# A fill of an unused tile after every gather on GpSimd, in a recommender kernel

## The chip, the cores and the metric

The kernel runs on one core of a Trainium2 chip. The metric is the device time of one execution in microseconds (us). The kernel before takes 5192.12 us, the median of three runs (5191.66 to 5192.24).

## The reference

The reference is a wide-and-deep recommender for a batch of 16384 examples. Each example looks up 32 rows of 300 floats in a table of 50000 words and takes their mean; it looks up 20 rows in each of three smaller tables (means) and one row in each of four small ones. The 748 features go through three dense layers, and a sum of scalar weights is added ahead of the sigmoid.

```python
tok = word_emb[token_idx].mean(axis=1)            # 32 rows of 300 floats
e1 = emb_mh1[mh1_idx].mean(axis=1)                # 20 rows of 64, also e2 and e3
o1 = emb_oh1[oh1_idx]                             # one row of 64, also o2, o3 and o4
emb = jnp.concatenate([tok, e1, e2, e3, o1, o2, o3, o4], axis=1)
wide = (wide_mh1[mh1_idx].sum(axis=(1, 2)) + ... + wide_oh4[oh4_idx][:, 0])[:, None]
h = jax.nn.relu(emb @ W1 + b1)                    # 748 -> 1024
h = jax.nn.relu(h @ W2 + b2)                      # 1024 -> 512
h = jax.nn.relu(h @ W3 + b3)                      # 512 -> 256
return jax.nn.sigmoid(h @ Wd + bd + wide)         # 256 -> 1
```

## The kernel before

The batch is cut into 128 tiles of 128 examples. Two streams of work run beside each other for each tile.

The token rows come from HBM. GpSimd issues one indirect DMA for each of the 32 token positions of a tile: 128 rows of 1200 bytes, one for each partition, 4096 gathers in all. Two gathers share one row buffer, and there are eight row buffers. VectorE adds the two halves of a buffer to a running sum in PSUM, three groups after the gathers of that buffer were issued.

```python
TOK_GROUP = 2
TOK_LAG = 3
TOK_BUFS = 8
...
tokp = ctx.enter_context(tc.tile_pool(name="tok", bufs=TOK_BUFS))
...
def add_up(t, q, rows):
    a, b = rows[:, 0:TOK_D], rows[:, TOK_D : 2 * TOK_D]
    if q == 0:
        nc.vector.tensor_add(tok_sum, a, b)
    else:
        nc.vector.tensor_add(tok_sum, tok_sum, a)                  # L216
        to = tok_sum
        if q == n_groups - 1:
            to = sums_of[t] = gp.tile([P, TOK_D], F32, name="g_tok")
        nc.vector.tensor_add(to, tok_sum, b)                       # L220

def tokens():
    under_way = []
    for n in range(n_all):
        if n < n_all - TOK_LAG:
            t, q = divmod(n, n_groups)
            it = token_indices[t // NSUB][:, t % NSUB, :].bitcast(U32)
            rows = tokp.tile([P, TOK_GROUP * TOK_D], F32, name="tok_rows")
            for r in range(TOK_GROUP):
                j = q * TOK_GROUP + r
                nc.gpsimd.indirect_dma_start(                      # L232
                    out=rows[:, r * TOK_D : (r + 1) * TOK_D],
                    out_offset=None,
                    in_=word,
                    in_offset=bass.IndirectOffsetOnAxis(ap=it[:, j : j + 1], axis=0),
                )
            under_way.append((t, q, rows))
        if n >= TOK_LAG:
            add_up(*under_way.pop(0))
        yield 1
```

The small tables are kept on chip. VectorE builds one-hot rows (L299), TensorE turns them into counts in PSUM tile `pc` (L317), ACT copies the counts to SBUF as fp8 (L324), and TensorE multiplies the counts with the tables into PSUM tile `pg` (L342). Every tile's features are then transposed by TensorE, tile by tile (`pt`), and the dense layers run on blocks of 256 examples (`ph`, L419, and the last layer `po`, L444).

The order of all this is written by hand: a loop over 11 steps per tile, and 16 steps more at the end, sends out a share of each stream in every step. The token groups are spread evenly over these steps, so that the groups of a tile drift against the tile's other work.

```python
n_steps = tiles * STEPS + WAKE
...
for step in range(n_steps):
    ...
    toks.to(n_all * (step + 1) / n_steps)
    for k in set(sums_of) - known:
        waiting.append((step + 2, Block.add_tokens, k, sums_of.pop(k)))
    ...
    if layers:
        layers.to(mlp_work * layers.size * (step + 1 - begin) / left + ahead)
```

Apart from four one-column constants, the identity for transposes and one row of numbers, GpSimd does nothing but these gathers.

Of the kernel before, what the change touches and what calls it, by code (L numbers as in the profile page):

```python
# [8 lines left out]
F32 = mybir.dt.float32  # L9
# [8 lines left out]
P = 128  # L18
# [4 lines left out]
TOK_GROUP = 2  # L23
TOK_LAG = 3
TOK_BUFS = 8
WAKE = 16
BLOCK = 512
LAYER_TILES = 2
# [20 lines left out]
def kernel(  # L49
# [21 lines left out]
    nc = tc.nc  # L71
# [11 lines left out]

    tokp = ctx.enter_context(tc.tile_pool(name="tok", bufs=TOK_BUFS))
    const = ctx.enter_context(tc.tile_pool(name="const", bufs=1))
# [108 lines left out]
    def load_weights():  # L194
# [7 lines left out]
        for sb, dram in ((wd_sb, wd), (b1_sb, b1), (b2_sb, b2), (b3_sb, b3), (bd_sb, bd)):  # L202
            nc.sync.dma_start(out=sb, in_=dram)

    n_groups = N_TOK // TOK_GROUP
    n_all = B // P * n_groups + TOK_LAG
    sums_of = {}
# [2 lines left out]
# [11 lines that stand above are left out]

    def tokens():

        under_way = []
        for n in range(n_all):
            if n < n_all - TOK_LAG:
# [8 lines that stand above are left out]
                        in_=word,  # L235
                        in_offset=bass.IndirectOffsetOnAxis(ap=it[:, j : j + 1], axis=0),
                    )
                under_way.append((t, q, rows))
            if n >= TOK_LAG:
                add_up(*under_way.pop(0))  # L240
            yield 1
# [255 lines left out]
    tiles = B // P  # L497
    n_steps = tiles * STEPS + WAKE
    mlp_work = NK * M1 + M1 * M2 + M2 * M3 + M3
# [19 lines left out]
    ctx.enter_context(tc.manual_schedule())  # L519
    ix = load_indices(0)  # L520
    toks = Paced(tokens())
    tables_on_chip = convert_tables()
    next(tables_on_chip)
# [96 lines left out]
```

## Time and profile before

| what | value |
|---|---|
| timed runs | 5192.12 us (median of 3) |
| the profiled execution | 7640.41 us, of which the span shown is 7638.6 us |
| mean granted TensorE clock in the profile | 0.875 |
| gathers | 4096, 629.41 MB in 196608 packets |
| share of 16 DMA engines that the gathers' packets took | 30.4% |

The profiled execution is much longer than the timed ones. So the durations of single instructions and the distances between them can be read from the profile, while shares of its span hold for that span alone. In the groups of the profile, each line gives the source line, the engine and the operation, what is written and read, the count, and then the busy time in us, the mean of one in ns, and the idle time of the engine just before, with what ended most of it. PE is TensorE's matmuls, PEld its weight loads, DVE is VectorE, ACT ScalarE and POOL GpSimd. In a timeline each line begins with the start and the duration in us.

### The profile page before, as it was taken

The numbers are of one execution on the slowest core, as the hardware profiler recorded it, in microseconds if no ns is written. First come the engines' busy times: TensorE is split into PE (matmuls) and PEld (weight loads), VectorE is DVE, ScalarE is ACT, GpSimd is POOL, SyncE is SP. The second block draws the span as 40 slices with busy tenths as digits, with TensorE's granted clock in tenths as the row PEclk, the third lists the DMA queues.
The fourth block names the chain that finished last, engine by engine and source line by source line (L and its number), as shares of the span: only waits on it lengthen the run. The fifth ranks groups of instructions, "written<-read, shape, count | busy, mean of one in ns | idle before, by whom it ended". The sixth has DMA issues, their size and how long they took to land.

```text
span 7638.6 us, 116204 instructions
## 1 busy us (share of the span) xinstructions
PE 5965.6 (78%) x46772; PEld 4692.2 (61%) x46772; DVE 3907.9 (51%) x8513; ACT 2574.7 (34%) x2403; POOL 3887.3 (51%) x4103
## 2 busy tenths in 40 slices
PE   4777777877777787877888888777778777777778
PEld 3656666666656666666666666666666666666667
DVE  6544454455544555545555555555545545454543
ACT  4333333333333333333333333333333333333332
POOL 6544454454554455555555555555555545444543
PEclk8888888888988888888888889898888988888889
DMA  5333333333333333333333333333333333333322
GB/s 147 86 81 84 82 84 82 83 86 82 84 84 83 82 86 86 83 86 84 88 88 85 88 87 90 88 86 86 87 85 86 87 81 83 81 81 82 85 80 64
DMA packets 253003, 653.37 MB, mean 86 GB/s; under 512 B 119040, under 2 KB 119617, under 8 KB 252461
## 3 DMA queue, kind: packets, MB, share of 16 engines
q0 software_dynamic: 196608, 629.41, 30.4%
q1 hardware_dynamic: 55853, 16.53, 1.0%
q8 instruction: 366, 6.00, 0.3%
q14 instruction: 176, 1.44, 0.1%
HBM read 645.59 MB, written 0.07 MB: 85 GB/s over the span
## 4 chain that ended last, share of the span: by engine, by line
PE 52%; another core or an unknown queue 19%; DVE 14%; issue 11%; ACT 4%; DVEq 0%; SPq 0%; DMA 0%; ACTq 0%
PE ph L419 24%; PE pg L342 17%; PE pc L317 8%; DVE own L216 4%; ACT cnt L324 4%; DVE slice L299 3%; DVE own L220 3%; DVE row L299 1%; PE po L444 1%; PE pt L387 1%; ACT h L428 1%; PE pt L403 1%; DVE g L348 0%; PE pt L384 0%
## 5 line engine op out<-in xcount | busy, mean ns | idle before, releaser
L232 POOL DMA_INDIRECT tok_rows<-in_word_emb_dram,it x4096 | 3886.4, 949 | 3711.7 <-DVE own L220 2388.0
L324 ACT ACTIVATE cnt<-pc 128x1656 fp8e3<-128x1656 f32 (+1 forms) x1408 | 2123.6, 1508 | 3163.7 <-remote 1568.4
L342 PE MATMUL pg<-terms,cnt 128*128 128x195 bf16 x17664 | 2187.3, 273 | 454.9 <-issue 394.1
L342 PEld LDWEIGHTS <-cnt 128*128 128x128 fp8e3 x17664 | 1805.4, 147 | 730.6 <-issue 612.7
L299 DVE TENSOR_TENSOR row<-own,sc 128x768 bf16<-128x768 bf16 (+1 forms) x1408 | 763.1, 542 | 1828.6 <-remote 1349.5
L317 PE MATMUL pc<-slice,row 64*128 64x138 bf16 x16384 | 824.6, 236 | 865.6 <-ACT cnt L324 336.1
L419 PE MATMUL ph<-h,w_sb 128*128 128x256 f32 (+1 forms) x5200 | 1395.8, 411 | 97.6 <-issue 90.4
L317 PEld LDWEIGHTS <-row 64*128 64x128 bf16 x16384 | 575.3, 100 | 1373.0 <-issue 1183.0
L419 PE MATMUL ph<-x_small,w_sb 128*128 128x256 f32 (+3 forms) x4160 | 1203.8, 418 | 85.2 <-issue 66.3
L419 PEld LDWEIGHTS ph<-h,w_sb 128*128 128x128 f32 x5200 | 1021.8, 210 | 277.9 <-issue 146.7
L428 ACT ACTIVATE h<-ph,b_sb 128x256 f32<-128x256 f32 (+1 forms) x910 | 427.6, 470 | 1813.5 <-remote 859.3
L419 PEld LDWEIGHTS ph<-x_small,w_sb 128*128 128x128 f32 (+1 forms) x4160 | 827.1, 213 | 236.9 <-issue 120.4
L216 DVE TENSOR_TENSOR own<-own,tok_rows 128x300 f32<-128x300 f32 x1920 | 917.0, 478 | 63.1
L348 DVE TENSOR_REDUCE g<-pg 128x130 f32<-128x390 f32 (+1 forms) x512 | 261.5, 511 | 1232.2 <-remote 515.9
L220 DVE TENSOR_TENSOR own<-own,tok_rows 128x300 f32<-128x300 f32 x1792 | 857.1, 478 | 61.8
L299 DVE TENSOR_TENSOR slice<-own,sc 128x828 bf16<-128x828 bf16 (+1 forms) x1408 | 797.0, 566 | 0.0
L419 PE MATMUL ph<-x_tok,w_sb 128*128 128x256 f32 (+1 forms) x2080 | 624.6, 407 | 23.1 <-issue 22.2
L419 PEld LDWEIGHTS ph<-x_tok,w_sb 128*128 128x128 f32 x2080 | 409.9, 209 | 88.0 <-issue 36.6
L405 DVE TENSOR_SCALAR x_tok<-pt 128x256 f32<-128x256 f32 x128 | 54.3, 424 | 338.3 <-PE pt L404 269.3
L388 DVE TENSOR_TENSOR x_small<-pt,scale 128x384 f32<-128x384 f32 x128 | 70.9, 554 | 104.3 <-PE pt L387 84.3
L444 PE MATMUL po<-h,wd_sb 128*1 128x256 f32 (+1 forms) x260 | 89.3, 470 | 37.4 <-ACT h L428 25.4
L403 PE MATMUL pt<-ident,g_tok 128*128 128x128 f32 x256 | 59.8, 316 | 28.1 <-ACT h L428 22.5
(43 smaller groups left out, 805.4 us busy)
## 6 DMA issues: line engine op xcount, KB each, us to landing
tok_rows<-in_word_emb_dram,it POOLq DMA_INDIRECT x4096
ix<-in_idx_dram SPq DMA_DIRECT2D x128, 32.0 KB
w_sb<-in_W_dram SPq DMA_DIRECT2D x6, 512.0 KB
raw<-in_mh_dram SPq DMA_DIRECT2D x3, 747.5 KB
it<-in_idx_dram SPq DMA_DIRECT2D x32, 64.0 KB
w_sb<-in_W_dram SPq DMA_DIRECT2D x1, 2048.0 KB
out_dram<-h SPq DMA_DIRECT2D x63, 1.0 KB
raw<-in_mh_dram SPq DMA_DIRECT2D x1, 617.5 KB
```

What stands on the lines that cost most here:

```text
L216: nc.vector.tensor_add(tok_sum, tok_sum, a)
L220: nc.vector.tensor_add(to, tok_sum, b)
L232: nc.gpsimd.indirect_dma_start(out=rows[:, r * TOK_D : (r + 1) * TOK_D], out_offset=None, in_=word, in_offset=bass.IndirectOffsetOnAxis(ap ...
L299: nc.vector.tensor_tensor(one[:, 0:rows, :].rearrange("p i (n d) -> p i n d", d=2), iota[:, 0:n].rearrange("p (n d) -> p n d", d=2).unsque ...
L317: nc.tensor.matmul(pc[:, f, k // n, at : at + n_h], hot[0][half, k, :], hot[1][half, k, :], start=True, stop=True,)
L324: nc.scalar.activation(cnt[:, :, b : b + rows, :].rearrange("l f (g k) h -> l f g (k h)", g=2), pc[:, :, :, 0 : n * n_h], AF.Copy, scale=0 ...
L342: nc.tensor.matmul(pg[:, j, :], by_slice[:, :, h], terms[:, h, :], start=(h == h0), stop=(h == h1 - 1))
L348: nc.vector.tensor_reduce(g[:, at : at + n * ROW].rearrange("p (f d) -> p f d", f=n), pg[:, 0:n, :].rearrange("p f (c d) -> p f d c", c=3) ...
L403: nc.tensor.transpose(pt[:, k, :], g[:, k * P : (k + 1) * P], ident)
L419: nc.tensor.matmul(ph[:, 0:n], weights[: src.shape[0], k, m * P : (m + 1) * P], src, start=(k == 0), stop=(k == len(srcs) - 1),)
L428: nc.scalar.activation(dst[:, m, 0:n], ph[:, 0:n], AF.Relu, bias=bias[:, m : m + 1])
L444: nc.tensor.matmul(po[:, 0:n], wd_sb[:, k : k + 1], h3[:, k, 0:n], start=(k == 0), stop=(k == M3 - 1))
```

## The change

After each gather GpSimd writes zeros to 256 columns of a tile that nothing reads. The fill computes nothing; it is there to put a pause between one gather and the next, so that they are spread in time. Nothing else is changed.

```diff
 TOK_BUFS = 8
+PAUSE = 256
 WAKE = 16
...
+    pause = const.tile([P, PAUSE], F32, name="pause")
     n_groups = N_TOK // TOK_GROUP
...
                     nc.gpsimd.indirect_dma_start(
                         out=rows[:, r * TOK_D : (r + 1) * TOK_D],
                         out_offset=None,
                         in_=word,
                         in_offset=bass.IndirectOffsetOnAxis(ap=it[:, j : j + 1], axis=0),
                     )
+                    nc.gpsimd.memset(pause, 0.0)
                 under_way.append((t, q, rows))
```

## The prediction, made before the changed kernel ran

> **What bounds the kernel now.** I read first the span against the timed runs. The profiled execution took 7638.6 us, the timed ones 5192.12 us, so the profile is stretched by 47% and shares of its span cannot be used as they stand; the durations and spacings of single instructions may. The head of the page and three groups:
>
> ```profile
> span 7638.6 us, 116204 instructions
> ...
> PE 5965.6 (78%) x46772; PEld 4692.2 (61%) x46772; DVE 3907.9 (51%) x8513; ACT 2574.7 (34%) x2403; POOL 3887.3 (51%) x4103
> ...
> L232 POOL DMA_INDIRECT tok_rows<-in_word_emb_dram,it x4096 | 3886.4, 949 | 3711.7 <-DVE own L220 2388.0
> L324 ACT ACTIVATE cnt<-pc 128x1656 fp8e3<-128x1656 f32 (+1 forms) x1408 | 2123.6, 1508 | 3163.7 <-remote 1568.4
> L342 PE MATMUL pg<-terms,cnt 128*128 128x195 bf16 x17664 | 2187.3, 273 | 454.9 <-issue 394.1
> ```
>
> The page makes GpSimd (POOL) look half idle: 3886.4 us busy, 3711.7 us idle. Two things say otherwise. Much of the stretch is waiting that the records cannot explain ("remote" in the ACT row, and 19% of the chain of waits goes to "another core or an unknown queue", though this is a one-core program); GpSimd then waits in turn for the row buffers that VectorE frees (2388.0 us on L220). And a gather costs more than its 949 ns. The timeline of GpSimd at the start, before any buffer is missing, has the columns start, duration, instruction, idle time before:
>
> ```profile
> 0.25 0.10 POOL L605 MEMSET const-float32-0.0<- 128x1 f32 x1 [0.25 <-issue]
> 0.28 0.10 POOL L605 MEMSET const-float32-1.0<- 128x1 f32 x1
> 0.30 0.11 POOL L605 MEMSET const-bfloat16-1.0<- 128x1 bf16 x1
> 0.33 0.12 POOL L605 MEMSET const-uint8-127<- 128x1 uint8 x1
> 0.74 0.20 POOL masks.py:197 MEMSET ident<- 128x128 f32 x1 [0.29 <-POOLq L605]
> ...
> 8.34 0.95 POOL L232 DMA_INDIRECT tok_rows<-in_word_emb_dram,it  x1 [0.30 <-issue]
> 9.59 0.95 POOL L232 DMA_INDIRECT tok_rows<-in_word_emb_dram,it  x1 [0.30 <-issue]
> 10.84 0.94 POOL L232 DMA_INDIRECT tok_rows<-in_word_emb_dram,it  x1 [0.30 <-issue]
> ```
>
> Gathers that wait for nothing start 1.25 us apart (8.34, 9.59, 10.84): 0.95 us recorded and 0.30 us "issue". No spacing in the whole trace is under 1.244 us. So 4095 spacings x 1.25 = 5119 us. The first gather starts at 3.15 us and the last one 40.0 us before the end of the span (7598.6 of 7638.6). Floor set by GpSimd: 3 + 5119 + 40 = **5162 us**, only 30 us (0.6%) under the timed 5192. I choose this as the bound: in the timed runs GpSimd issues gathers practically without a break, and the three runs agree within 0.6 us, as a fixed instruction rate would give.
>
> TensorE is close behind. In the timeline of TensorE:
>
> ```profile
> 3009.24 0.54 PE L317 MATMUL pc<-slice,row 64*128 64x138 bf16 x12
> 3009.72 1.52 PE L342 MATMUL pg<-terms,cnt 128*128 128x195 bf16 x15
> 3011.07 1.92 PE L419 MATMUL ph<-h,w_sb 128*128 128x256 f32 x8
> ...
> 3019.18 2.78 PE L419 MATMUL ph<-h,w_sb 128*128 128x256 f32 x12
> 3021.90 0.42 PE L317 MATMUL pc<-slice,row 64*128 64x138 bf16 x8
> ```
>
> From start to start, 12 matmuls into pc take 0.48 us (0.040 each), 15 into pg 1.35 (0.090), 12 layer matmuls 2.72 (0.227). With the counts of the page, 16384 x 0.040 + 17664 x 0.090 + 11440 x 0.227 = 655 + 1590 + 2597 = 4842 us, plus my estimate of 200 us for transposes and the last layer: about 5040 us. That is 3% under the time[...].
>
> [...] 0.205 us for 128 columns (the group's mean) against 0.098 us for one gives 107 / 127 = 0.84 ns per column.[...] I add nothing for VectorE; no run here shows it yet.[...] The trace has a mean granted clock of 0.875 in the stretched span[...].
>
> **The change part by part.** Removed: nothing. Moved: nothing; on the other four engines the built program has the same number of instructions as before. Added: a constant tile of 1 KB per partition, and 4096 MEMSETs of 128x256 f32, so that GpSimd's stream goes from one gather after another to gather, fill, gather, fill. Each fill waits for the semaphore of the fill before it, which ended a whole gather earlier; that costs no time. No gather waits for a fill's semaphore.[...]
> - Columns: 256 x 0.84 = 0.215 us.
> - Handing over: the one-column fills start 0.025 to 0.03 us apart, so about 0.025 us beside the columns. Sum 0.24 us.
> - Upper figure:[...] the whole duration counts: 0.098 + 255 x 0.84 ns = 0.312 us.
>
> None of it lies beside other work, since GpSimd is the bound and the fill sits in its queue: 4096 x 0.24 = 983 us, 4096 x 0.312 = 1278 us. New times 5192 + 983 = 6175 and 5192 + 1278 = 6470. I take 0.255 us, nearer the lower: 4096 x 0.255 = 1045, **6240 us**, 20% more. GpSimd then needs 1.505 us per gather and every other engine has slack: TensorE's 5040 us fit in 6240[...].
>
> **The rivals.**
> 1. *The fill disappears in the 0.30 us between gathers.*[...] a fill of 0.24 us fits and the time stays near 5192. For it: the gap is called "issue", and it is about as long as the fill. Against it: after a true wait for a buffer the semaphore instruction is followed by a gather 0.22 us later, less than 0.30, and where a gather is preceded by a semaphore instruction that does not wait, the spacing is 1.25 all the same.[...] Half hidden, 0.12 us per gather would give 5690.
> 2. *TensorE is the bound in timed runs and gathers have slack without the profiler.* If the 0.30 us is an effect of recording, a gather costs 0.95 us, the floor is 3900 us, and with the fill 4096 x 1.19 = 4880: nothing happens. For it: TensorE's 5040 us. Against it: it takes a coincidence for 4096 x 1.25 to come within 0.6% of the time.
> 3. *The fill costs more than its columns*, because each gather after a different instruction starts cold. The first gather has 1.10 us against 0.95, 0.15 us more. If a part of that returned each time, a fill would cost 0.35 us or more: 5192 + 4096 x 0.35 = 6626.
> 4. *Spacing out the gathers speeds something up.* The page's DMA row has the gather queue at 30.4% of 16 engines' span, about 45% of the timed 5192; there is nothing to relieve there, and nothing the pause could shorten lies on the path.
>
> **Range and chances.** From rival 1 partly true, 0.15 us per gather (5192 + 614 = 5806), to rival 3, 0.34 us (5192 + 1393 = 6585): 5800 to 6600. Fully hidden or TensorE-bound: 8% and 6%, together 14% for the same time. Faster needs a shorter gather, for which nothing speaks: 2%. Slower: 84%.
>
> **What would show it.** The GpSimd timeline of the changed kernel should show undisturbed gathers about 1.5 us apart, each with a MEMSET between; near 1.25 means rival 1, 1.6 rival 3. The group of fills should have about 310 ns. Gather duration should stay 0.95 us. Waits of GpSimd for the adds that free row buffers (L220) should shrink, since gathers come slower and buffers are free earlier; in their place TensorE, ACT and VectorE should wait more for rows. The profiled span should grow by much less than 1000 us, as part of the fills falls into waits that only the profiled execution has. The prediction fails[...] if the gather spacing differs without the profiler.

## The result and the profile after

The changed kernel takes **5990.7 us** (three runs, 5989.56 to 5991.6) against 5192.12 us, a ratio of 1.1538 with an interval of 1.1512 to 1.1564. That is 798.6 us more, or 0.195 us for each of the 4096 fills. The page of the changed kernel, with the same parts as the lines shown of before (busy us, share of the span, count; then groups with busy us, mean ns and idle us):

```profile
span 5988.9 us, 120300 instructions
...
PE 5293.3 (88%) x46772; PEld 4316.5 (72%) x46772; DVE 3862.8 (64%) x8513; ACT 2604.7 (43%) x2403; POOL 5250.5 (88%) x8199
...
POOL 56%; DMA 15%; DVE 11%; issue 9%; PE 9%; POOLq 0%; ACT 0%; DVEq 0%; SPq 0%; ACTq 0%
...
L235 POOL DMA_INDIRECT tok_rows<-in_word_emb_dram,it x4096 | 3914.0, 956 | 706.7 <-issue 604.3
L328 ACT ACTIVATE cnt<-pc 128x1656 fp8e3<-128x1656 f32 (+1 forms) x1408 | 2124.4, 1509 | 1879.9 <-PE pc L321 1871.2
L346 PE MATMUL pg<-terms,cnt 128*128 128x195 bf16 x17664 | 1843.1, 254 | 429.8 <-DVE g L352 428.7
...
L241 POOL MEMSET pause<- 128x256 f32 x4096 | 1345.5, 328 | 2.7
```

The chain that ended last now runs through GpSimd (56%) and the rows that it fetches (DMA, 15%). The gathers last as long as before (956 ns against 949) and hardly wait for row buffers: 604.3 of the 706.7 us ahead of them are "issue", and no wait for VectorE among the rest is over 0.2 us. The fills are charged with 1345.5 us, far more than the 798.6 us that they cost. In GpSimd's timeline (start, duration, idle before):

```profile
3007.89 0.95 POOL L235 DMA_INDIRECT tok_rows<-in_word_emb_dram,it  x1 [0.17 <-issue]
3008.84 0.33 POOL L241 MEMSET pause<- 128x256 f32 x1
3009.33 0.95 POOL L235 DMA_INDIRECT tok_rows<-in_word_emb_dram,it  x1 [0.17 <-issue]
3010.28 0.33 POOL L241 MEMSET pause<- 128x256 f32 x1
3010.78 0.95 POOL L235 DMA_INDIRECT tok_rows<-in_word_emb_dram,it  x1 [0.17 <-issue]
```

Gather to gather it is 1.44 us (the median over the whole trace is 1.444), against 1.251 before. 0.193 x 4096 = 791 us, close to the 798.6 us measured; the experiments on the bound show that the sum closes less neatly than this. A recorded fill of 0.33 us lengthens the spacing by 0.19 us only, because the gap ahead of a gather shrinks from 0.30 to 0.17.

One thing did not fit. The profile of before was 7638.6 us long, that of after is 5988.9 us, the same as its timed runs. The stretch that the prediction laid at the profiler's door was gone. The runs below show where it came from. They fell on three chips, here called by their numbers 6, 8 and 14; each run is compared with the kernel before on the same chip. For the runs up to here the record names no chip; 5192.12 us is like chip 6 below (5191.73 us), the profile's 7640.41 us like chip 8 (7638.91 us).

### The profile page after: what moved, and what is told of

It is laid out like the page before. It is cut to its first block, busy times and chain, and to the rows that moved or that the text cites. A ratio compares the mean times of both kernels' runs of the same rounds, so it can differ in the third digit from the quotient of the medians.

```text
span 5988.9 us, 120300 instructions
## 1 busy us (share of the span) xinstructions
PE 5293.3 (88%) x46772; PEld 4316.5 (72%) x46772; DVE 3862.8 (64%) x8513; ACT 2604.7 (43%) x2403; POOL 5250.5 (88%) x8199
## 4 chain that ended last, share of the span: by engine, by line
POOL 56%; DMA 15%; DVE 11%; issue 9%; PE 9%; POOLq 0%; ACT 0%; DVEq 0%; SPq 0%; ACTq 0%
POOL tok_rows L235 42%; DMA tok_rows<-in_word_emb_dram,it 15%; POOL pause L241 14%; PE ph L423 5%; DVE own L222 3%; DVE row L303 2%; PE pg L346 2%; DVE g L352 1%; DVE own L218 1%; DVE slice L303 1%; PE pc L321 1%; PE po L448 0%; POOLq L235 0%; DVE wide_row L396 0%; DVE g_tok L222 0%
## 5 line engine op out<-in xcount | busy, mean ns | idle before, releaser
L235 POOL DMA_INDIRECT tok_rows<-in_word_emb_dram,it x4096 | 3914.0, 956 | 706.7 <-issue 604.3
L346 PE MATMUL pg<-terms,cnt 128*128 128x195 bf16 x17664 | 1843.1, 254 | 429.8 <-DVE g L352 428.7
L346 PEld LDWEIGHTS <-cnt 128*128 128x128 fp8e3 x17664 | 1617.5, 144 | 467.9 <-issue 337.6
L222 DVE TENSOR_TENSOR own<-own,tok_rows 128x300 f32<-128x300 f32 x1792 | 857.3, 478 | 1040.1 <-DMA tok_rows<-in_word_emb_dram,it 1017.5
L241 POOL MEMSET pause<- 128x256 f32 x4096 | 1345.5, 328 | 2.7
L423 PE MATMUL ph<-h,w_sb 128*128 128x256 f32 (+1 forms) x5200 | 1304.8, 397 | 7.7 <-DVE x_small L410 7.7
L423 PE MATMUL ph<-x_small,w_sb 128*128 128x256 f32 (+3 forms) x4160 | 1121.6, 400 | 20.8 <-DVE x_small L410 12.5
L423 PEld LDWEIGHTS ph<-h,w_sb 128*128 128x128 f32 x5200 | 984.5, 202 | 182.5 <-issue 59.2
L321 PEld LDWEIGHTS <-row 64*128 64x128 bf16 x16384 | 502.0, 95 | 651.6 <-issue 262.7
L321 PE MATMUL pc<-slice,row 64*128 64x138 bf16 x16384 | 758.9, 224 | 164.9 <-DVE slice L303 135.0
L216 DVE TENSOR_TENSOR own<-tok_rows 128x300 f32<-128x300 f32 x128 | 61.3, 479 | 187.6 <-DMA tok_rows<-in_word_emb_dram,it 187.3
L222 DVE TENSOR_TENSOR g_tok<-own,tok_rows 128x300 f32<-128x300 f32 x128 | 60.2, 471 | 74.2 <-DMA tok_rows<-in_word_emb_dram,it 72.7
```

What stands on the lines that cost most here:

```text
L235: nc.gpsimd.indirect_dma_start(out=rows[:, r * TOK_D : (r + 1) * TOK_D], out_offset=None, in_=word, in_offset=bass.IndirectOffsetOnAxis(ap ...
L241: nc.gpsimd.memset(pause, 0.0)
L321: nc.tensor.matmul(pc[:, f, k // n, at : at + n_h], hot[0][half, k, :], hot[1][half, k, :], start=True, stop=True,)
L346: nc.tensor.matmul(pg[:, j, :], by_slice[:, :, h], terms[:, h, :], start=(h == h0), stop=(h == h1 - 1))
L423: nc.tensor.matmul(ph[:, 0:n], weights[: src.shape[0], k, m * P : (m + 1) * P], src, start=(k == 0), stop=(k == len(srcs) - 1),)
```

## Experiments on the price of a fill (chip 6, kernel before 5191.73 us)

**One column.** Theory A is the prediction's: a fill adds to GpSimd's time between two gathers, by its columns. Theory B is a fixed price for any instruction between two gathers.

```diff
-PAUSE = 256
+PAUSE = 1
```

> One column in each fill in place of 256; 4096 fills as before. Theory A (a fill adds[...] by its columns, at about 0.84 ns each, less a small part that hides in the gap between gathers): gathers stay at 1.25 us and the time is within 1% of 5192 us. Theory B (a fixed price of having another instruction between two gathers, whatever its size): gathers 1.44 us apart and about 5990 us, as with 256 columns.

Measured: 5219.99 us, ratio 1.0054 (1.0037 to 1.0071). GpSimd's timeline:

```profile
2999.34 0.95 POOL L235 DMA_INDIRECT tok_rows<-in_word_emb_dram,it  x1 [0.19 <-issue]
3000.29 0.11 POOL L241 MEMSET pause<- 128x1 f32 x1
3000.60 0.95 POOL L235 DMA_INDIRECT tok_rows<-in_word_emb_dram,it  x1 [0.19 <-issue]
```

A fill of 0.11 us is there, and gathers still start 1.25 us apart (median 1.251): it fits into the gap. Theory B falls. The 28 us that remain are not in the median spacing: in this trace 65 gathers follow the one before by over 0.1 us more than the median, together 61 us. The chain that ended last is 76% TensorE, which is 97% busy. There is no trace of the kernel before on chip 6 to compare with, so what the 28 us are stays open.

**128 columns.**

```diff
-PAUSE = 256
+PAUSE = 128
```

> 128 columns in each fill. Theory A: 128 x 0.84 = 0.107 us less for each fill than with 256, so 1.444 - 0.107 = 1.337 us per gather and 5991 - 440 = 5550 us. Theory B: 5990 us. If half or more of the 0.30 us gap could take fills in for nothing, it would be 5192 us.

Measured: 5564.88 us, ratio 1.0716 (1.0699 to 1.0734), spacing 1.339 us, as theory A has it. So half of the gap cannot take fills in for nothing.

**Twice the elements in the same bytes.**

```diff
-PAUSE = 256
+PAUSE = 512
...
-    pause = const.tile([P, PAUSE], F32, name="pause")
+    pause = const.tile([P, PAUSE], BF16, name="pause")
```

> 512 columns of bf16 in each fill: twice the elements in the same bytes. If a fill is priced by element (theory A as it stands): 1.444 + 0.215 = 1.66 us per gather and 5991 + 881 = 6870 us. If by bytes: 1.444 us and 5991 us.

Measured: 6847.87 us, ratio 1.3189 (1.3167 to 1.3211), spacing 1.659 us. At this size a fill is priced by element, not by byte.

**Two fills of 128.**

```diff
-                    nc.gpsimd.memset(pause, 0.0)
+                    nc.gpsimd.memset(pause[:, 0 : PAUSE // 2], 0.0)
+                    nc.gpsimd.memset(pause[:, PAUSE // 2 : PAUSE], 0.0)
```

> Two fills of 128 columns after each gather in place of one of 256: the same columns and twice the instructions. Theory A: about 0.03 us of handing over on top, 1.47 us per gather, 6100 us at most. Theory B (a fixed price for each instruction): up to 1.25 + 2 x 0.195 = 1.64 us and 6790 us.

Measured: 6123.91 us, ratio 1.1795 (1.1775 to 1.1815), spacing 1.477 us: 0.033 us more than one fill of 256. That is the price of one more instruction, a little over the 0.03 us and the 6100 us that theory A gave.

The spacings lie on one line:

| columns | 1 | 128 | 256 | 512 |
|---|---|---|---|---|
| measured spacing, us | 1.251 | 1.339 | 1.444 | 1.659 |
| 1.229 + 0.00084 per column | 1.230 | 1.337 | 1.444 | 1.659 |

Only the first point is off: with one column the spacing is 1.251 us, as it is without a fill. By this line, which the points at 256 and 512 give, some 0.02 us of a fill, about 25 columns, is free, and each further column costs 0.84 ns; how wide a fill can be before it costs anything was not measured between 1 and 128 columns.

## Experiments on what bound the kernel before

**Fewer layer matmuls.** GpSimd's part stays and TensorE's shrinks.

```diff
     for m in range(n_out):
         ph = ps_h.tile([P, N], F32, name="ph", tag="ph")
+        srcs = srcs[:1]
         for k, src in enumerate(srcs):
```

It leaves out 9620 of the 11440 layer matmuls.

> The kernel before, without fills, with each dense layer summing only its first chunk of features (one matmul for each output chunk in place of 4 to 8): 9620 of the 11440 layer matmuls are left out, some 2200 us of TensorE at 0.227 us each. If gathers bind the kernel before (theory A): 5192 us within 1%. If TensorE binds it and gathers have slack without the profiler: well below 5000 us.

Measured: 7136.48 us. But the kernel before, unchanged, took 7561.89 us in the same session (ratio 0.9447, 0.9415 to 0.9478). This chip, 14, is one where the kernel before itself takes half as long again, without a profile too. So the question was left open until the same kernel ran on chip 6:

> The kernel before with most layer matmuls left out, once more. On a chip where the kernel before takes 5192 us: if GpSimd's gathers are a second bound just under TensorE's, 5165 to 5180 us (3 + 4095 x 1.251 + 40 us, and the few longer spacings); if TensorE alone sets 5192 us, below 5000 us. On a chip where the kernel before takes over 7500 us: 7136 us as the first time, and nothing is told apart.

Measured: **5154.98 us** on chip 6, against 5191.73 for the kernel before, ratio 0.9929 (0.9907 to 0.9952). With TensorE 69% busy the time falls by 0.7% and no further; spacing 1.251 us. Its page:

```profile
span 5153.2 us, 96841 instructions
...
PE 3540.7 (69%) x37152; PEld 2846.0 (55%) x37152; DVE 3863.9 (75%) x8513; ACT 2587.3 (50%) x2403; POOL 3887.1 (75%) x4103
```

The first gather starts at 3.11 us; 4095 spacings of 1.251 us make 5123 us, longer spacings add 10 us, and the last gather starts 17.4 us before the end: 5153 us. That is GpSimd's own bound. It is 10 us below the range expected, which took 40 us for the end.

**Half of the gathers, without and with fills.** One gather for each pair, its rows added twice; half of the token rows are left out.

```diff
-        a, b = rows[:, 0:TOK_D], rows[:, TOK_D : 2 * TOK_D]
+        a = b = rows[:, 0:TOK_D]
...
-                for r in range(TOK_GROUP):
+                for r in range(1):
```

> The kernel before, without fills, with one gather for each pair: half of the token rows are left out, and each gathered row is added twice in the place of two rows. VectorE and TensorE do the same work as before. GpSimd then needs 2048 x 1.25 = 2560 us. Theory A: the time falls to what TensorE needs, 4850 to 5050 us, by the estimate of about 5040 us. If TensorE bound the kernel before: 5192 us still.

> The same with one gather for each pair, and a fill of 256 columns after each: GpSimd needs 2048 x 1.444 = 2957 us. Theory A: GpSimd is not the bound, so fills cost nothing, the same time as with half of the gathers and no fill within 1%. Theory C (fills disturb VectorE[...], whoever binds): over 2% slower than without fills, and longer VectorE instructions.

Measured on chip 14: **5193.57 us** without fills, 5187.26 us with one of 256 columns after each gather. The page of the first:

```profile
PE 5073.6 (98%) x46772; PEld 4161.2 (80%) x46772; DVE 3908.1 (75%) x8513; ACT 2594.0 (50%) x2403; POOL 1945.3 (37%) x2055
...
PE 95%; DVE 3%; issue 1%; ACT 0%; DMA 0%; another core or an unknown queue 0%; SPq 0%; DVEq 0%; ACTq 0%
```

TensorE is 98% busy and makes up 95% of the chain: 5190 us is TensorE's own bound. The 4850 to 5050 us of theory A were too low; of the two cases, "5192 us still" came true. Two engines thus bound the kernel before (where it takes 5192 us), TensorE at about 5190 us and GpSimd at 5155 us. With half of the gathers GpSimd binds nothing and the fills cost nothing. VectorE's additions last as long without them (first line) as with them (second):

```profile
L216 DVE TENSOR_TENSOR own<-own,tok_rows 128x300 f32<-128x300 f32 x1920 | 917.1, 478 | 63.0
L218 DVE TENSOR_TENSOR own<-own,tok_rows 128x300 f32<-128x300 f32 x1920 | 917.1, 478 | 63.0
```

Theory C, fills in VectorE's way, falls.

With the two bounds known, the result adds up like this: GpSimd's own 5155 us and 791 us for the fills make 5946 us. The other 45 us stand in the traces of the changed kernel and of the one with fewer matmuls: spacings longer than the median (43 us in all against 10), and 29.8 us against 17.4 from the last gather to the end. That 791 us came within 8 us of the measured difference was luck, for two errors cancel: the 37 us by which TensorE's bound lies above GpSimd's, and these 45 us.

## Experiments on the long runs (chips 8 and 14)

**The kernel before once more, with a profile.** No edit.

> The kernel before, unchanged, profiled once more. If the stretch of its profile (7638.6 us against 5192) belongs to the pace of its gathers under the profiler, it is stretched again; fills of one column, which leave the gathers at 1.25 us, had a profile of 5218 us, so a stretch that comes and goes would show about 5200 us here.

Measured: 7536.52 us on chip 14, beside timed runs of 7532.57 to 7581.71. So the stretch is not the profiler's. It seems to go with the chip: every run of this kernel on chip 6 took 5191 to 5194 us, in two sets of runs. Chips 8 and 14 were seen in one set each, so there chip and time cannot be told apart. The lower granted clock does not explain it: if all of TensorE's 5190 us (at a clock of 0.997) stretched with the 0.879 of this run, that would be some 5900 us, by estimate. The timeline shows the stretch at work:

```profile
3004.75 0.95 POOL L232 DMA_INDIRECT tok_rows<-in_word_emb_dram,it  x1 [0.30 <-issue]
...
3006.65 0.24 PE L342 MATMUL pg<-terms,cnt 128*128 128x195 bf16 x1 [0.37 <-issue]
3007.25 0.95 POOL L232 DMA_INDIRECT tok_rows<-in_word_emb_dram,it  x1 [0.30 <-issue]
...
3008.75 0.32 PE L342 MATMUL pg<-terms,cnt 128*128 128x195 bf16 x1 [0.37 <-issue]
...
3010.16 1.53 PE L342 MATMUL pg<-terms,cnt 128*128 128x195 bf16 x8 [0.32 <-issue]
3010.31 0.47 ACT L428 ACTIVATE h<-ph,b_sb 128x256 f32<-128x256 f32 x1 [7.29 <-remote]
3010.40 0.56 DVE L299 TENSOR_TENSOR row<-own,sc 128x768 bf16<-128x768 bf16 x1 [6.84 <-remote]
...
3012.76 0.94 POOL L232 DMA_INDIRECT tok_rows<-in_word_emb_dram,it  x1 [4.56 <-DVE own L220]
```

GpSimd has been issuing gathers every 1.25 us since 2999.76. At about 3004.5 TensorE falls from many matmuls a microsecond to one or two every 0.7 us; ACT and VectorE stand for 7 us for reasons the records do not name ("remote"). GpSimd, getting no row buffer back, stops after the gather at 3007.25 (4.56 us of waiting on L220); about 3 us later, from 3010.2 on, all go on, with eight matmuls in 1.53 us. Over the whole trace I counted the time that TensorE lost in gaps over 0.5 us between two matmul starts, by the place of the last gather in an unbroken run of gathers (spacings up to 1.45 us, or 1.7 us with fills of 256; the first gather of a run has place 0):

```
place in the run                      0-3          4      5      6-7    8-9
kernel before, chip 14, us lost    0.09 to 0.16   0.38   1.13   1.50   1.28   per gather
256 columns, chip 8, us lost       0.05 to 0.13   0.27   0.39   0.62   0.98   per gather
```

The table alone does not tell cause from effect, for a hold-up of any cause can starve GpSimd of buffers (in this trace it waits 2294.9 us on L220, in 660 waits) and so end its run. The next table therefore counts only the first gap of each run: of the runs that have come to a place without a gap, the share that has one there.

```
place in the run                       0-3           4      5      6
kernel before, chip 14, share    0.04 to 0.10      0.24   0.62   0.75
256 columns, chip 8, share       0.04 to 0.08      0.21   0.32   0.43
1 column, chip 6, share          0.07 to 0.14      0.06   0.03   0.03
```

On chips 8 and 14 the risk of a hold-up grows with the length of the run, and more slowly when the gathers are further apart; on chip 6 it does not grow. With half of the gathers only 4 of 1368 runs are longer than four gathers, and the hold-ups are gone.

On chip 6 a run of 1-column fills goes on for over 60 gathers at the same 1.25 us and loses 0.02 us per gather at places 21 to 60. The gathers themselves are no slower on either kind of chip: from the start of a gather to its last packet, the median is 2.53 to 2.55 us in all these traces. Nor are their single packets slower: the median is 0.184 us on chips 6 and 14 alike. That of the instruction queue's large packets is 1.00 us on chip 6 (1-column fills) and 1.09 us on chip 14 (kernel before).

**The changed kernel and 1-column fills, on chip 8.** No further edit; the kernel before takes 7638.91 us there.

> The changed kernel once more, to see it on a chip where the kernel before takes 7560 us (the chip that runs this is not ours to choose). Theory D (more than about four gathers back to back at 1.25 us hold up all other engines there, and a fill breaks the run of gathers): 5990 us on either chip, so 21% faster than the kernel before where that takes 7560 us. Theory E (such a chip slows whatever gathers all rows, fills or not): over 7500 us there. Where the kernel before takes 5192 us: 5990 us, and nothing is told apart.

> Fills of one column once more, for the same reason. They leave the gathers 1.25 us apart. If spacing is what matters (theory D): about 7500 us where the kernel before takes 7560 us, and 5220 us where that takes 5192 us. If any other instruction between two gathers is enough: 5220 us on either chip.

Measured: **7014.05 us** with 256 columns, ratio 0.918 (0.915 to 0.9209), and 7720.87 us with one column, ratio 1.0105 (1.0062 to 1.0148). On chip 8 the change makes the kernel 8% faster, not 15% slower. Another instruction between two gathers is not enough, for the 1-column fill, which leaves gathers at 1.25 us, does not help (1.0105); the fill of 256 columns, which widens the spacing, does (0.918). But theory D as I put it, 5990 us on either chip, falls with theory E: the hold-ups come later and cost less, and they do not go away. Waits of the changed kernel on chip 8 (us in total, times, longest):

```profile
ACT cnt L328 <- remote: 1295.9, 371, 11.5
PEld L321 <- issue: 1099.4, 1430, 5.6
POOL tok_rows L235 <- DVE own L222: 1001.4, 447, 7.4
```

GpSimd still waits 1001.4 us for row buffers, where in the profile before it was 2388.0 us, and that is nearly the difference between 7014 and 5991 us.

**512 columns once more.** The question is whether wider spacing takes the rest of the hold-ups away.

> Fills of 512 columns once more, gathers 1.66 us apart. On a chip where the kernel before takes over 7500 us, theory D read as a budget that refills (other engines are held up after about five gathers at 1.25 us and about seven at 1.44, which would make some 1.95 us per gather what can be kept up): hold-ups come later still, GpSimd waits for little, and the time is 6850 to 7150 us. If fills no longer help at that size: GpSimd's 6850 us plus as much waiting as with 256 columns, some 7850 us. On a chip where the kernel before takes 5192 us: 6848 us.

Measured: 6846.73 us on chip 6, as the first time. Wider spacing on a chip like 8 or 14 was not seen, so the budget that refills, with its 1.95 us per gather, remains an estimate from the places of the hold-ups. How the gathers hold up the other engines, and why chips 8 and 14 show it and chip 6 does not, stays open; no run here separates the issuing on GpSimd from the traffic of the rows.

## Why the prediction was right, and where not

- **Time and direction** held: 5990.7 us lies between 5800 and 6600, and the mechanism is the one written down, fills in series with gathers on GpSimd.
- **The mis-sized term** is "None of it lies beside other work". The columns were right: 256 x 0.84 = 0.215 us, and 0.84 ns per column was measured up to 512. To this I added 0.025 us for handing over and then leaned towards the full duration, 0.255 us in all, 6240 us. The measured price is 0.193 us of spacing, less than the columns alone. An added instruction does cost 0.033 us, as two fills of 128 show. If the first fill costs that too, 0.215 + 0.033 - 0.193 = 0.055 us of it lies in the gap ahead of the next gather; what is measured without this assumption is the sum, 0.02 us less than the columns. Counting the recorded 0.328 us for each fill would have been worse still: 1345 us.
- **Rival 1**, the fill disappears in the gap, is true of some 25 columns of 256.
- **The bound.** That GpSimd is the bound and TensorE close behind had the order wrong: TensorE at 5190 us comes ahead of GpSimd at 5155 us. Rival 2 was right that TensorE is the bound, wrong that gathers have slack; the coincidence that I held against it is what happened. That three runs agree within 0.6 us was no sign of GpSimd's rate either: with TensorE as the bound and half of the gathers, four runs agree within 1.4 us. The count of gathers gave 5162 us for GpSimd's floor, within 0.2% of 5155. The sum over matmuls gave 5040 us for TensorE, 3% too low: in the trace with half of the gathers the matmuls take, from start to start, 703 us into `pc`, 1629 into `pg`, 2617 into `ph` and 232 for the rest, against my 655, 1590, 2597 and 200. In its first 100 us TensorE does only 449 of 46772 matmuls and is busy for 42 us; steady stretches do not show that. For the change the order made no difference, since GpSimd had only some 35 us to spare.
- **What was assumed without a run.** That nothing need be added for VectorE: its additions take 478 ns with fills and without. That TensorE has slack: in the changed kernel it is 88% busy at a granted clock of 0.959 and makes up 9% of the chain. That the fills' waits for one another cost nothing: the idle time ahead of all 4096 fills is 2.7 us.
- **Two sums** are a few us off, without effect: in rival 1, 5192 + 4096 x 0.12 is 5684 and not 5690; in rival 2, 4096 x 1.19 is 4874 and not 4880.
- **Rival 4**, that spacing the gathers speeds something up, was given 2% and was right where I could not see it: on chip 8. "Nothing the pause could shorten lies on the path" was wrong for the very trace in hand, in which GpSimd's 2388.0 us of waiting and TensorE's single matmuls were hold-ups of that kind. I took them for the profiler's doing and left them out, so the profile before and the time before came from two different behaviours of the kernel. That the prediction held is luck in this: it was measured where the kernel before takes 5192 us, and on chip 8 the same change has the ratio 0.918. By the same step failed "the profiled span should grow": it shrank by 1650 us.
- The gathers' duration, the fills in between, and the waits moving to VectorE's adds for rows (1017.5 us on L222 alone) came as foretold; the recorded fills have 328 ns against 310, and the spacing is 1.444 us against 1.5.

## What to carry to other kernels

Find the price of an instruction on GpSimd from start-to-start spacing, and change its size once or twice to split it into a fixed part and a part per element; the recorded duration of a fill was 0.328 us here and its price 0.193 us. When a profile is much longer than the timed runs, time the same kernel without the profiler on the chip that the profile came from, before calling it the profiler's doing: here a pause that costs 15% on one chip earns 8% on another. Before a wait is weighed, take away the work of one engine at a time: two such kernels showed two bounds 35 us apart that the profile before had not told apart.

## What the runs showed of the hardware that I had not expected

- A gather of 128 rows of 1200 bytes occupies GpSimd for 1.25 us (1.251 on chips 6 and 14, 1.252 with a 1-column fill on chip 8), and its last packet ends 2.53 us after its start in the median, also late in the runs of chip 14, where the other engines are held up.
- On chips 8 and 14 TensorE, ACT and VectorE are held up together (ACT for 7.29 us and VectorE for 6.84 us in the timeline of chip 14) after about four gathers back to back: of the runs that come to place 4 without a gap, the share that has one there is 0.24 on chip 14 (kernel before, 1.25 us apart) and 0.21 on chip 8 (256 columns, 1.44 us apart), against 0.04 to 0.10 and 0.04 to 0.08 at places 0 to 3. On chip 14 TensorE then loses 1.13 to 1.50 us for each gather at places 5 to 9. With half of the gathers (5193.57 us on chip 14) it is gone.
- A fill of 512 bf16 columns costs about twice a fill of 256 f32 columns, at the same bytes (spacing 0.408 us longer against 0.193).
